# Layer 3's attention: a head's scores on 64 rows in one pass, heads two at a time, operands stacked through device memory, four attentions issued as one stream

## The chip, the core and the metric

The kernel runs on one core of one Trainium2 chip. The metric is the device time of one launch in microseconds. A core has a matrix engine (TensorE, PE in the profile; its weight loads are PEld), a vector engine (VectorE, DVE), a scalar engine (ScalarE, ACT), GpSimd (POOL), and a queue that issues transfers (SyncE, SP). Each engine works through its own instructions in order; semaphores tie them together. On-chip memory is SBUF, the matrix engine writes to PSUM, and device memory is HBM.

## The reference

Four layers in a row are added to a tensor `x` of 2 x 128 x 64 x 64 in float32; each takes the group-normalised tensor. Layers 0 to 2 (an attention with a channel attention, a convolution mix, a quaternion Fourier layer) are the same before and after. Layer 3 is a plain self-attention over the 4096 positions, with 8 heads of 16 channels, for each of the two batch entries:

```python
    xf = x.reshape(B, C, S)                      # 2, 128, 4096
    q, k, v = proj(wq, bq), proj(wk, bk), proj(wv, bv)   # each B, 8, 16, S
    a = jnp.einsum('bhcq,bhck->bhqk', q, k) / jnp.sqrt(jnp.float32(C))
    a = jax.nn.softmax(a, axis=-1)
    o = jnp.einsum('bhqk,bhck->bhcq', a, v)
    return o.reshape(B, C, h, w)                 # added to x
```

## The kernel before, in words

**The work of layer 3.** It is cut into four attentions: batch entry `b` (0, 1) times a set `t` (0, 1) of four heads, `j` = 0 to 3. In each, the queries are cut into 8 blocks `qb` of 512 columns (`CH`, `NCH`) and the keys into 32 tiles `kt` of 128 (`NQT`). One step is one (`qb`, `kt`): there are 256 steps in an attention and 1024 in the layer. A step is

- `scores` (L2102): for every head a 128 x 512 block of scores into PSUM, keys on the partitions. Two PSUM tiles `ps_s` hold it, heads 0 and 1 in the first, heads 2 and 3 in the second. There are three such tiles in the pool (`f3_sp`, `bufs=3`), so a step's pair shares a buffer with its neighbours;
- two exponentials on ScalarE (L2112), 128 x 1024 each, from `ps_s` to `weights` in SBUF;
- `multiply` (L2121): for every head `weights` times the 32 columns of `vt` (16 channels of values and 16 of ones, whose sums are the softmax's denominators), four heads beside each other in 32-column strips of the array, summed over `kt` in one PSUM tile `ps_acc`. It runs two steps behind `scores`.

At the last `kt` of a block `done` (L2141 to L2154) transposes, divides, adds the residual and writes out.

**How a score is split.** Scores are computed in the fast float32 form of TensorE (`F32R`, "fp32r" in the profile) from rounded parts, so that nothing is lost. A head has 32 rows: 16 channels twice. In `k` the upper copy holds the rounded key and the lower one its remainder (`hi`, `sign`, `upper`); in `q[0]` both copies hold the rounded query, in `q[1]` its remainder. Head `j` sits on rows 32j to 32j+31, so four heads work side by side in the array, and a step takes two passes: all four heads with `q[0]`, then all four with `q[1]`, added up in PSUM.

**Around it.** `folded` folds the normalisation of batch entry `b` into the weights (its statistics by `_group_stats_pow`). `queries_and_keys` makes `q` and `k` by pieces of 512 columns: a matmul (L2030), then seven VectorE operations; for the first two pieces of all, three of them are on ScalarE. `values` (L2056, L2063) makes `vt` in 8 pieces, each 4 matmuls and one VectorE addition. `bound` takes the largest query and key for a flag, checked at the end of the kernel.

**What sets the order.** Inside layer 3 `_in_order` keeps PE, DVE, ACT and POOL in the order of the program text; the SP queue is ordered by the framework's scheduler. The first attention starts when two pieces of queries, keys and values are there; the other pieces follow inside its first block, one at every second `kt` (`early`). Each attention carries the preparation of the next one beside it (`beside`): one piece at `kt` = 4, 12 and 20 of a block, 16 pieces with a matmul each or four, and some more without. An attention ends with `for x in waiting: multiply(*x)`, then the next one begins.

Of the kernel before, what the change touches and what calls it, by code (L numbers as in the profile page):

```python
# [1288 lines left out]
F32R = mybir.dt.float32r  # L1289
ENGINES = (  # L1290
# [672 lines left out]
def _layer3(ctx, tc, X, l3, cst, out, worst, here):  # L1963
# [10 lines left out]
    def acc():  # L1974
        return accp.tile([128, CH], F32, tag="acc", name="ps_acc")
# [11 lines left out]
    def folded(b, got):  # L1987

        x = X[:, b, :]
        if b:  # L1990
            mean, rstd = _group_stats_pow(nc, two, acc, x, cst, mhalf)
        else:
            mean, rstd = here[:, 0:1], here[:, 1:2]
        yield
# [24 lines left out]
    def queries_and_keys(b, t, f, q, k, idle):  # L2019

        wqk, _, bqk, _ = f
        bq, bk, bk2 = (bqk[:, n, t : t + 1] for n in range(3))
        for c in range(NCH):
            cols = slice(c * CH, (c + 1) * CH)
            ps = acc()
            nc.tensor.matmul(ps, wqk[:, t, :], X[:, b, cols], start=True, stop=True)  # L2030

            qq = two.tile([128, CH], F32, tag="qq", name="qq", bufs=1)
            nc.vector.stream_shuffle(qq, ps, OF_Q)  # L2033
            kk = two.tile([128, CH], F32, tag="kk", name="kk", bufs=1)
            nc.vector.stream_shuffle(kk, ps, OF_K)  # L2035
            hi = two.tile([128, CH], F32R, tag="hi", name="hi", bufs=1)
            if c < idle:
                nc.scalar.activation(hi, kk, AF.Identity, bias=bk)
                nc.scalar.activation(kk, kk, AF.Identity, bias=bk2, scale=upper)  # L2039
                nc.scalar.activation(q[0][:, cols], qq, AF.Identity, bias=bq)  # L2040
            else:
                nc.vector.tensor_scalar_add(hi, kk, bk)
                nc.vector.tensor_scalar(kk, kk, bk, upper, ALU.add, ALU.mult)
                nc.vector.tensor_scalar_add(q[0][:, cols], qq, bq)
            nc.vector.scalar_tensor_tensor(k[:, cols], hi, sign, kk, ALU.mult, ALU.add)
            nc.vector.scalar_tensor_tensor(
                q[1][:, cols], qq, bq, q[0][:, cols], ALU.add, ALU.subtract
            )
            yield
# [20 lines left out]
    def bound(b, t, q, k):  # L2070


        top = two.tile([128, 2, 2], F32, tag="top", name="top")
        for n, x in enumerate((q[0], k)):
            for i in range(2):
                nc.vector.tensor_reduce(
                    top[:, n, i : i + 1],
                    x[:, i * S // 2 : (i + 1) * S // 2],
                    AX.X,
                    ALU.max,  # L2080
                    apply_absolute_value=True,
                )
                yield
        m = two.tile([128, 2], F32, tag="m", name="m")
        nc.vector.tensor_reduce(m, top, AX.X, ALU.max)
        mm = two.tile([128, 1], F32, tag="mm", name="mm")
        nc.vector.scalar_tensor_tensor(mm, m[:, 0:1], lower, m[:, 1:2], ALU.mult, ALU.mult)
        ps = acc()
        nc.tensor.matmul(ps[:, 0:1], head_sum, mm, start=True, stop=True)  # L2089
        n = 1 + 2 * b + t  # L2090
        nc.vector.tensor_scalar_mul(worst[:, n : n + 1], ps[:, 0:1], 1.02)
        yield

    def attend(b, t, q, k, vt, early):
        ac = [None]

        def scores(qb, kt):
            ps = [spp.tile([128, 2, CH], F32, tag="sp", name="ps_s") for _ in range(2)]
            for n in range(2):
                for j in range(4):  # L2100
                    rows = slice(32 * j, 32 * j + 32)
                    nc.tensor.matmul(  # L2102
                        ps[j // 2][:, j % 2, :],
                        k[rows, kt * 128 : (kt + 1) * 128],
                        q[n][rows, qb * CH : (qb + 1) * CH],
                        start=(n == 0),
                        stop=(n == 1),
                    )
            w = []
            for p in range(2):  # L2110
                w.append(pp.tile([128, 2, CH], F32, tag="weights", name="weights"))
                nc.scalar.activation(w[p], ps[p], AF.Exp)  # L2112
            return w

        def multiply(qb, kt, w):
            if kt == 0:
                ac[0] = acc()
            for j in range(4):

                i = j % 2  # L2120
                nc.tensor.matmul(  # L2121
                    ac[0][32 * j : 32 * j + 32, :],
                    vt[:, kt, j // 2, i : i + 2, :].rearrange("p a d -> p (a d)"),
                    w[j // 2][:, i, :],
                    start=(kt == 0),
                    stop=(kt == NQT - 1),
                )
            if kt == NQT - 1:
                done(qb, ac[0])

        def done(qb, ps):
            cols = slice(qb * CH, (qb + 1) * CH)

            places = [
                (slice(32 * j + 16 * (j % 2), 32 * j + 16 * (j % 2) + 16),
                 slice(64 * t + 16 * j, 64 * t + 16 * j + 16))
                for j in range(4)
            ]
            xs = residual[qb % 2]
            for to, rows in places:  # L2140
                nc.sync.dma_start(xs[to, :], X[rows, b, cols])  # L2141
            z = two.tile([128, CH // 32, 32], F32, tag="z", name="z", bufs=1)
            flat = z.rearrange("p n i -> p (n i)")
            nc.vector.transpose(flat, ps)  # L2144
            r = two.tile([128, CH // 32], F32, tag="r", name="r")
            for j in range(4):
                rows = slice(32 * j, 32 * j + 32)
                nc.vector.reciprocal(r[rows, :], z[rows, :, 16 * (1 - j % 2)])  # L2148
            nc.vector.tensor_mul(z, z, r.unsqueeze(2).to_broadcast([128, CH // 32, 32]))
            u = two.tile([128, CH], F32, tag="u", name="u", bufs=1)  # L2150
            nc.vector.transpose(u, flat)
            nc.vector.tensor_add(u, u, xs)
            for at, rows in places:
                nc.sync.dma_start(out[b, rows, cols], u[at, :])  # L2154

        waiting = []
        for qb in range(NCH):
            for kt in range(NQT):
                if kt % 2 == 0:
                    over = next(early, early) is early  # L2160
                waiting.append((qb, kt, scores(qb, kt)))
                if len(waiting) > 2:
                    multiply(*waiting.pop(0))
                yield kt if over else None
        for x in waiting:
            multiply(*x)
# [10 lines left out]
    def work():  # L2177

        for b in range(B):
            f = []  # L2180
            yield from folded(b, f)
            for t in range(2):
                first = b == 0 and t == 0
                q = [two.tile([128, S], F32R, tag=f"q{n}", name=f"q{n}") for n in range(2)]
                k = two.tile([128, S], F32R, tag="k", name="k")
                vt = two.tile([128, NQT, 2, 3, 16], F32, tag="vt", name="vt")
                early = values(b, t, f, vt)
                keys = queries_and_keys(b, t, f, q, k, 2 * first)
                if first:

                    for _ in range(2):
                        next(keys)
                        next(early)
                        yield
                    early = in_turn(keys, early)
                else:
                    for _ in early:
                        yield
                    yield from keys
                yield b, t, (q, k, vt, early)  # L2200
                yield from bound(b, t, q, k)

    def up_to_next(side):
        for x in side:
            if x:
                found.append(x)
                return
            yield

    side = work()  # L2210
    found = []
    for _ in up_to_next(side):
        pass
    while found:
        b, t, got = found.pop()
        beside = up_to_next(side)
        for kt in attend(b, t, *got):

            if kt in (4, 12, 20):
                next(beside, None)  # L2220
        for _ in beside:
            pass


def _input(nc, X, a, b):
    for i in range(4):
# [127 lines left out]
```

## Time and profile before

| what | value |
|---|---|
| median of 3 runs | 4194.57 us (4191.61 to 4198.47) |
| the profiled execution's own time | 4192.35 us |
| its span | 4190.2 us |
| layer 3 in it: first exponential to the end of the last | 2233.1 to 4178.0 us |
| exponentials of layer 3 | 2048, busy 1884.9 us, idle before them 61.0 us |
| PE busy over the span | 96% |
| ACT busy over the span | 80% |

How to read the profile: the busy time of an engine is the union of its instructions' times, so that 2048 exponentials of 1101 ns each, which overlap a little, are busy for 1884.9 us. A matmul's end is modelled, and matmuls overlap, so that a busy PE says nothing of how much of it is needed; what it waits for is read from its weight loads (PEld). "idle before" with an arrow is the time for which the engine stood still before such instructions, and what came last to release it. In the timeline "x8" means eight instructions of a kind in a row, and a time in brackets is the idle time before the first of them.

### The profile page before, as it was taken

Reading aid. Unit: us, or ns where it says so; the run is one execution under the profiler, and the core shown is the slowest. Engines: PE = TensorE matmul, PEld = TensorE weight load, DVE = VectorE, ACT = ScalarE, POOL = GpSimd, SP = SyncE. Lnnn points to the kernel's source line nnn. Section 1 sums busy time; section 2 is a strip of 40 time slices with the busy share of each in tenths; the row PEclk is TensorE's granted clock in tenths of the full one; section 3 lists DMA queues with packets and bytes.
Section 4 is the critical chain, followed back from the end, with each engine's and each line's share of the span. In section 5 each row is a group of like instructions: output and inputs, shape, how many; then the busy total and the mean of one; then the engine's idle time right before and its main releaser. Section 6 shows DMA issues by size and latency. Waiting matters only on the chain. (4 is left out here: it accounts for less than half of the span.)

```text
span 4190.2 us, 90476 instructions
## 1 busy us (share of the span) xinstructions
PE 4027.6 (96%) x39886; PEld 1505.7 (36%) x39886; DVE 2088.3 (50%) x2454; ACT 3333.8 (80%) x4035; POOL 71.7 (2%) x145
## 2 busy tenths in 40 slices
PE   7999999989999998997999999999999999999998
PEld 4522222354222224445664333333333333333333
DVE  4689999767899998895754102221022102210000
ACT  4478888735888883326646999999999999999998
POOL 1001000000000001000000000000000000000000
PEclk9999999999999999998989999999999999999999
DMA  1199970000000000004640000000000000000000
GB/s 49 26 185 181 179 98 1 2 2 2 1 2 2 2 2 12 1 15 190 271 195 4 6 6 6 4 6 6 4 6 6 6 4 6 6 4 6 6 6 5
DMA packets 158855, 159.39 MB, mean 38 GB/s; under 512 B 24809, under 2 KB 148713, under 8 KB 154354
## 3 DMA queue, kind: packets, MB, share of 16 engines
q1 hardware_dynamic: 158450, 153.50, 15.7%
q8 instruction: 314, 5.14, 0.5%
q14 instruction: 91, 0.75, 0.1%
HBM read 145.09 MB, written 73.40 MB: 52 GB/s over the span
## 5 line engine op out<-in xcount | busy, mean ns | idle before, releaser
L2112 ACT ACTIVATE weights<-ps_s 128x1024 f32<-128x1024 f32 x2048 | 1884.9, 1101 | 61.0 <-PE ps_s L2102 60.6
L1352 ACT ACTIVATE weights<-ps_s 128x1024 f32<-128x1024 f32 x1024 | 993.1, 1023 | 167.9 <-PE ps_s L1343 149.7
L2121 PE MATMUL ps_acc<-weights,vt 128*32 128x512 f32 x8192 | 1093.2, 606 | 0.0
L2102 PE MATMUL ps_s<-q,k 32*128 32x512 f32 x8192 | 924.1, 444 | 5.4 <-ACT weights L2112 5.4
L1800 DVE TENSOR_TENSOR sums<-sums,weights 128x2048 f32<-128x2048 f32 x384 | 880.0, 2292 | 42.6 <-ACT weights L1352 6.4
L2102 PEld LDWEIGHTS ps_s<-q,k 32*128 32x128 f32 x8192 | 471.2, 182 | 839.7 <-ACT weights L2112 773.1
L1343 PE MATMUL ps_s<-q,k 32*64 32x512 f32 x8192 | 629.9, 613 | 4.6 <-ACT weights L1352 2.4
L1760 PE MATMUL ps_acc<-weights,vt 128*32 128x512 f32 x4096 | 550.0, 605 | 7.2 <-ACT used L1790 3.7
L2144 DVE STREAM_TRANSPOSE z<-ps_acc 128x512 f32<-128x512 f32 x32 | 22.9, 717 | 1064.6 <-PE ps_acc L2121 1064.6
L1343 PEld LDWEIGHTS ps_s<-q,k 32*64 32x64 f32 x8192 | 161.5, 129 | 433.9 <-PE ps_s L1343 337.9
L2121 PEld LDWEIGHTS ps_acc<-weights,vt 128*32 128x32 f32 x8192 | 162.9, 108 | 378.6 <-issue 375.4
L1760 PEld LDWEIGHTS ps_acc<-weights,vt 128*32 128x32 f32 x4096 | 81.2, 108 | 426.7 <-issue 403.2
L662 DVE SCALAR_TENSOR_TENSOR X<-g,w,X 128x2048 f32<-128x2048 f32 x84 | 197.4, 2351 | 2.6
L1800 DVE TENSOR_TENSOR sums<-weights 128x2048 f32<-128x2048 f32 x64 | 146.6, 2291 | 63.0 <-ACT weights L1352 62.6
L1548 PE MATMUL ps_sp<-pad,diag 32*32 32x512 f32 x4608 | 158.9, 597 | 2.3 <-ACT q L1568 1.3
L1008 PE MATMUL ps_z<-w_ri,e 128*32 128x128 f32 x2048 | 137.5, 409 | 14.5 <-DVE e L950 12.3
L2063 DVE TENSOR_TENSOR vt<-ps_acc,bv 128x384 f32<-128x384 f32 x32 | 17.8, 557 | 264.7 <-PE ps_acc L2056 264.7
L2033 DVE LOAD_MASK_SELECT qq<-ps_acc x32 | 0.4, 14 | 239.0 <-PE ps_acc L2030 239.0
L1548 PEld LDWEIGHTS ps_sp<-pad,diag 32*32 32x32 f32 x4608 | 95.5, 103 | 53.6 <-issue 15.6
L950 DVE TENSOR_SCALAR e<-ps_pe 32x136 f32<-32x136 f32 (+1 forms) x352 | 104.4, 297 | 4.9
L948 ACT ACTIVATE e<-ps_pe 32x136 f32<-32x136 f32 (+1 forms) x352 | 99.3, 282 | 4.1
L710 PE MATMUL ps_bank<-t,t 128*128 128x512 f32 x224 | 101.3, 610 | 0.0
(288 smaller groups left out, 2488.6 us busy)
## 6 DMA issues: line engine op xcount, KB each, us to landing
w_ri<-w_r SPq DMA_DIRECT2D x16, 2112.0 KB, 8.1
w_ri<-w_i SPq DMA_DIRECT2D x16, 2112.0 KB, 13.4
w_r<-in_L_conv_kr_w SPq DMA_DIRECT2D x15, 528.0 KB, 13.1
w_r<-in_L_conv_kr_x SPq DMA_DIRECT2D x15, 528.0 KB, 12.9
w_r<-in_L_conv_kr_y SPq DMA_DIRECT2D x15, 528.0 KB, 12.9
w_r<-in_L_conv_kr_z SPq DMA_DIRECT2D x15, 528.0 KB, 12.9
w_i<-in_L_conv_ki_w SPq DMA_DIRECT2D x15, 528.0 KB, 13.3
w_i<-in_L_conv_ki_x SPq DMA_DIRECT2D x15, 528.0 KB, 12.7
```

Of the source, the lines that this page charges most:

```text
L662: nc.vector.scalar_tensor_tensor(xi, g[:, i : i + H // 2, j : j + W], w8[:, s : s + 1], xi, ALU.mult, ALU.add)
L710: nc.tensor.matmul(ps.rearrange("p (h w) -> p h w", w=W), t9[:, k, :], t2[:, c * ROWS + k : (c + 1) * ROWS + k, 2 : W + 2], start=(k == 0) ...
L950: nc.vector.tensor_scalar_mul(out, got[of, :, s], sign)
L1008: nc.tensor.matmul(out.rearrange("p (n f o) -> p n f o", n=2, f=2), e[:, s, 2 * j : 2 * j + 2, :].rearrange("p f x -> p (f x)"), w.rearran ...
L1343: nc.tensor.matmul(ps[j // 2][to, j % 2, :], k[rows, kt * 128 + 64 * half : kt * 128 + 64 * half + 64], q[rows, qb * CH : (qb + 1) * CH], ...
L1352: nc.scalar.activation(w[:, 2 * p : 2 * p + 2, :], ps[p], AF.Exp)
L1548: nc.tensor.matmul(ps[r // 2][to, r % 2, :].rearrange("p (h w) -> p h w", w=W), diag[rows, grp, t, :], pad[rows, y0 : y0 + ROWS, t % 3 : t ...
L1760: nc.tensor.matmul(ac[n][rows, :], lhs(rows), w[:, j, :], start=first, stop=last)
L1800: nc.vector.tensor_add(parts[0].rearrange("p j c -> p (j c)"), t.rearrange("p j c -> p (j c)"), w.rearrange("p j c -> p (j c)"),)
L2102: nc.tensor.matmul(ps[j // 2][:, j % 2, :], k[rows, kt * 128 : (kt + 1) * 128], q[n][rows, qb * CH : (qb + 1) * CH], start=(n == 0), stop= ...
L2112: nc.scalar.activation(w[p], ps[p], AF.Exp)
L2121: nc.tensor.matmul(ac[0][32 * j : 32 * j + 32, :], vt[:, kt, j // 2, i : i + 2, :].rearrange("p a d -> p (a d)"), w[j // 2][:, i, :], star ...
```

## The change

The parts, with the names of the diff:

1. `scores`: a head's 64 rows (16 channels, times two parts of the query, times two parts of the key) are multiplied in one pass. Rows 0 to 63 and 64 to 127 take a head each, so two heads work at a time: heads 0 and 1, then heads 2 and 3. A step has 4 score matmuls of 64 rows instead of 8 of 32 rows, and 4 weight loads of 64 x 128 instead of 8 of 32 x 128. Every matmul starts and stops its own sum.
2. `queries_and_keys` writes each piece's three 128 x 512 tiles (`q[0]`, `q[1]`, `k`) to device memory (3 transfers of 256 KB), and `stacked` reads them back so that the rows of `q[0]` and `q[1]` alternate and those of `k` stand twice: 8 transfers of 64 rows x 512 (128 KB each). Queries and keys are held as 8 + 8 single tiles of 128 x 2 x 512 instead of two sets of three 128 x 4096 tiles; the next attention's tiles take the places of those which the present one has finished with (`laid`).
3. The maximum for `bound` is taken piece by piece inside `queries_and_keys` (2 reductions of 512 columns for each piece) instead of 4 reductions of 2048 afterwards.
4. The four attentions run as one stream: `waiting` goes on across them, so that the last multiplies of one come after the first scores of the next. Preparation is laid at `kt` = 3, 6, ..., 30 of a block (`SIDE`), taking `others` (bound, fold, values, statistics) and `keys` in turn. A piece of queries and keys is four such turns, of which only the first has a matmul. `keys` of the next attention begin in its second block. The statistics of the second batch entry come by `_stats_steps`.
5. An exponential on VectorE (`exponentials`) is written, but `BY_VECTOR` is empty, so it is not used, and `ORDER` is the plain order.

```diff
-    def queries_and_keys(b, t, f, q, k, idle):
...
-                nc.vector.tensor_scalar_add(q[0][:, cols], qq, bq)
-            nc.vector.scalar_tensor_tensor(k[:, cols], hi, sign, kk, ALU.mult, ALU.add)
-            nc.vector.scalar_tensor_tensor(
-                q[1][:, cols], qq, bq, q[0][:, cols], ALU.add, ALU.subtract
+    def queries_and_keys(g, c, idle):
...
+        nc.vector.stream_shuffle(kk, ps, OF_K)
+        yield
+        k = two.tile([128, CH], F32R, tag="ks", name="ks", bufs=1)
+        q = [two.tile([128, CH], F32R, tag=f"qs{n}", name=f"qs{n}", bufs=1) for n in range(2)]
...
+        yield
+        nc.vector.scalar_tensor_tensor(k, k, sign, kk, ALU.mult, ALU.add)
+        nc.vector.scalar_tensor_tensor(q[1], qq, bq, q[0], ALU.add, ALU.subtract)
+        for n, x in enumerate((q[0], q[1], k)):
+            to = dram.tile([128, CH], F32, name=f"stack{2 * b + t}_{c}_{n}")
+            nc.sync.dma_start(to, x.bitcast(F32))
+            g.kept[c, n] = to
+        yield
+        for n, x in enumerate((q[0], k)):
+            nc.vector.tensor_reduce(
+                top[:, n, c : c + 1], x, AX.X, ALU.max, apply_absolute_value=True
             )
-            yield
+        yield
+
+    def stacked(g, c, name, parts):
+
+        to = one.tile([128, 2, CH], F32R, tag=f"{name}{c}", name=f"{name}{c}")
+        for n, part in enumerate(parts):
+            for p in range(2):
+                nc.sync.dma_start(
+                    to[n::2, p, :].bitcast(F32), g.kept[c, part][64 * p : 64 * p + 64, :]
+                )
+        getattr(g, name)[c] = to
...
-            for n in range(2):
-                for j in range(4):
-                    rows = slice(32 * j, 32 * j + 32)
-                    nc.tensor.matmul(
-                        ps[j // 2][:, j % 2, :],
-                        k[rows, kt * 128 : (kt + 1) * 128],
-                        q[n][rows, qb * CH : (qb + 1) * CH],
-                        start=(n == 0),
-                        stop=(n == 1),
-                    )
...
+    def scores(g, qb, kt):
+        ps = [spp.tile([128, 2, CH], F32, tag="sp", name="ps_s") for _ in range(2)]
+        keys = slice(kt % 4 * 128, kt % 4 * 128 + 128)
+        for j in range(4):
+            rows = slice(64 * (j % 2), 64 * (j % 2) + 64)
+            nc.tensor.matmul(
+                ps[j // 2][:, j % 2, :],
+                g.k[kt // 4][rows, j // 2, keys],
+                g.q[qb][rows, j // 2, :],
+                start=True,
+                stop=True,
+            )
...
-        for kt in attend(b, t, *got):
-
-            if kt in (4, 12, 20):
-                next(beside, None)
-        for _ in beside:
...
+    def attended(g, early, others, following):
+
+        after, over, keys = None, False, iter(())
+
+        def laid(qb, kt):
+
+            for name, parts, free in (("q", (0, 1), qb), ("k", (2, 2), kt // 4 if qb == NCH - 1 else 0)):
+                c = len(getattr(after, name))
+                if c < free and (c, 2) in after.kept:
+                    stacked(after, c, name, parts)
+
+        for n in range(NCH * NQT):
+            qb, kt = divmod(n, NQT)
+            if kt % 2 == 0:
+                over = next(early, early) is early
+            next(chain[0], None)
+            scores(g, qb, kt)
+            waiting.append((g, qb, kt))
+            if len(waiting) > LAG:
+                multiply(*waiting.pop(0))
+            if after:
+                laid(qb, kt)
+            if not over or kt not in SIDE:
+                continue
+            if SIDE.index(kt) % 2 == 0:
+                next(others, None)
+                continue
+            if after is None and following and qb:
+                for _ in others:
+                    pass
+                after, others = following()
+                keys = chained(*after.keys)
+            next(keys, None)
...
+    def first_laid(keys, g):
+
+        for c in range(NCH):
+            yield from keys[c]
+            stacked(g, c, "q", (0, 1))
+            stacked(g, c, "k", (2, 2))
+
+    f = []
+    run(folded(0, here, f))
+    g = Group(0, 0, f, 2)
+    keys = in_pieces(first_laid(g.keys, g), 4)
+    for c in range(2):
+        next(keys)
+        next(g.values)
+    early = in_turn(keys, g.values)
```

## The prediction

> **What bounds the kernel now.** I read the groups of instructions first, then busy time by attention, then the timeline in a quiet stretch and around a piece of preparation, and last the start of layer 3. The change touches only layer 3, so nothing before 2220 us should move.
>
> ```profile
> L2112 ACT ACTIVATE weights<-ps_s 128x1024 f32<-128x1024 f32 x2048 | 1884.9, 1101 | 61.0 <-PE ps_s L2102 60.6
> L2121 PE MATMUL ps_acc<-weights,vt 128*32 128x512 f32 x8192 | 1093.2, 606 | 0.0
> L2102 PE MATMUL ps_s<-q,k 32*128 32x512 f32 x8192 | 924.1, 444 | 5.4 <-ACT weights L2112 5.4
> ```
>
> ScalarE is the bound: 2048 exponentials, idle for 61.0 us, all but 0.4 of it waiting for scores. PE looks busier (1093.2 + 924.1), but these are overlapping, modelled times. The windows, ACT's exponentials alone, one row for each attention (columns: stretch, length, busy and count, granted clock, DMA share, GB/s):
>
> ```profile
> 2233.00:2733.00 500.00, 475.75 (x516) 1.00 0.02 5
> 2733.00:3222.00 489.00, 471.04 (x513) 1.00 0.02 6
> 3222.00:3710.00 488.00, 471.32 (x513) 1.00 0.02 6
> 3710.00:4178.00 468.00, 466.78 (x509) 1.00 0.02 6
> ```
>
> Idle: 24, 18, 17 and 1 us. The last attention, which prepares no successor, loses nothing; the others lose it to preparation, and the first also to its own start.
>
> ```profile
> 3899.08 5.71 ACT L2112 ACTIVATE weights<-ps_s 128x1024 f32<-128x1024 f32 x6
> ...
> 3900.08 0.47 PEld L2102 LDWEIGHTS ps_s<-q,k 32*128 32x128 f32 x8 [0.84 <-ACT weights L2112]
> ...
> 3900.92 0.16 PEld L2121 LDWEIGHTS ps_acc<-weights,vt 128*32 128x32 f32 x8 [0.37 <-issue]
> ...
> 3901.92 0.47 PEld L2102 LDWEIGHTS ps_s<-q,k 32*128 32x128 f32 x8 [0.84 <-ACT weights L2112]
> ```
>
> Quiet: a step takes 1.833 us (two exponentials at a pitch of 0.917). Scores start at 3900.08, and the exponential that needs them at 3899.08 + 2 x 0.917 = 3900.91, 0.83 later. So PE has no lead. Now a stretch with one piece:
>
> ```profile
> 2239.53 1.13 PE L2030 MATMUL ps_acc<-X,wqk 128*128 128x512 f32 x2
> 2240.59 0.30 PEld L2102 LDWEIGHTS ps_s<-q,k 32*128 32x128 f32 x8 [0.76 <-ACT weights L2112]
> 2241.26 0.16 PEld L2121 LDWEIGHTS ps_acc<-weights,vt 128*32 128x32 f32 x8 [0.37 <-issue]
> 2241.42 3.77 ACT L2112 ACTIVATE weights<-ps_s 128x1024 f32<-128x1024 f32 x4 [0.85 <-PE ps_s L2102]
> 2242.25 0.54 PEld L2102 LDWEIGHTS ps_s<-q,k 32*128 32x128 f32 x8 [0.84 <-issue]
> ...
> 2729.53 7.44 ACT L2112 ACTIVATE weights<-ps_s 128x1024 f32<-128x1024 f32 x8 [1.87 <-PE ps_s L2102]
> ```
>
> A piece occupies PE for 1.06 us (2239.53 to 2240.59). Unhindered scores take 0.67 (to 2241.26), the multiply 0.99 (to 2242.25): PE needs 1.66 of 1.83, 0.17 to spare. The exponential came 0.85 late. The last row is the seam between two attentions.
>
> The loss to be won: from 2233.13 to 4177.96 are 1944.8 us, less 1024 x 1.833 = 1877: 68 us. Pieces: 3 x 16 at 0.97 = 47 (0.85 idle, and some 0.1 because exponentials no longer overlap). The first block: 12 pieces, one at every second step, about 13. The seams, 3 x 2.3: 7. Sum 67.
>
> **The change, part by part.**
>
> *Scores.* PE time: before, two passes of four heads, 0.67, so 0.335 for one. After, two passes of two heads with 512 columns each. No row shows a matmul on 64 rows. Nearest is the 32-row pass, 0.335; the low end is 0.30, for fewer loads; the high end, if two heads don't overlap, is four times 0.335 = 1.34 a step. I take 0.67: the time is in the columns. [...] all eight loads, the second pass's on the same rows, were over in 0.30, while matmuls of 0.44 mean ran. [...]
>
> *What is gained is the lead.* Before, both PSUM tiles were complete only after the second pass, 0.83 after the start, and both had to be free for the first pass to finish. After, heads 0 and 1 finish in the first pass: their exponential can start at 0.83 - 0.335 = 0.50; I take 0.59, since a first pass also waits for its weights. The second tile need only be free when the second pass starts. Let e be the start of an exponential: its tile is free at e + 1.17 (1.12 for the late exponentials and a semaphore), the second pass starts at e + 1.28, PE is through at e + 1.615, the multiply at e + 2.605, and the next pair's first exponential could start at e + 3.195. ScalarE reaches it at e + 4 x 0.917 = e + 3.667. Lead: 0.47, before 0.
>
> So a piece of 1.06 costs ScalarE 0.59 instead of 0.97. The lead comes back at 0.17 a step, so in three steps: the smallest distance in `SIDE`. 48 x 0.59 = 28. In the first block pieces come every second step and 0.34 is rebuilt: 12 x 0.72 = 9. Together 37.
>
> *One stream.* At a seam the next scores precede the last multiplies: 7 becomes 0. Bound, fold and statistics have matmuls of 0.3 to 0.4 a turn and fit the lead.
>
> Exponentials win 68 - 37 = 31 us.
>
> *Stacks, at the start.* This is what the change adds to the path.
>
> ```profile
> 2221.70 4.97 SPq L2141 DMA_DIRECT2D residual<-X  x8
> ...
> 2231.87 1.57 PE L2102 MATMUL ps_s<-q,k 32*128 32x512 f32 x10
> ...
> 2233.13 7.44 ACT L2112 ACTIVATE weights<-ps_s 128x1024 f32<-128x1024 f32 x8 [1.11 <-PE ps_s L2102]
> ```
>
> The transfers nearest in size (KB each, median us from issue to landing):
>
> ```profile
> out<-u SPq DMA_DIRECT2D x128, 32.0 KB, 1.7
> ...
> w_k<-in_L_conv_wk SPq DMA_DIRECT2D x1, 128.0 KB, 2.1
> ```
>
> SP takes 0.62 to issue one (4.97 / 8), [...] I take 0.5. The first piece's `q[1]` is ready at 2228.1 (L2046 at 2227.32, 0.74 long). A 256 KB store: above the 2.1 of 128 KB, say 2.4; the last, issued by 2228.9, has landed at 2231.3. Eight loads from 2229.7 on, one every 0.5: issued by 2233.7, landed 2.1 later at 2235.8. Scores start 3.9 later than 2231.87, the first exponential some 3 later, since it needs one pass only. The next piece's `ks`, `qs` wait for stores to have left: 1 more. Cost 4. PE does a piece (1.06) meanwhile, inside this wait: back 1. Net 3; ends 2 and 20.
>
> The upper end is the loop in the first block: every four steps a piece goes through SP, 3 stores, landing, 8 loads. At 0.5 and 2.4 about 8 us, against 4 x 1.66 + 2 x 1.06 = 8.8 for PE: hidden. At 0.62 and 4.7 (the 512 KB input's landing) it is 11.5: 2.7 late, six times, 16.
>
> *Costed at nothing.* Later stacks: SP has a block of 58.7 us for about 11 transfers more, and tiles are asked for at least 20 us ahead of use; 56 MB over 1900 us is 30 GB/s, where earlier stages of this kernel moved 190 to 270. SP is in order, so `out` and `residual` stand behind stores that wait for VectorE and loads that wait for PE to leave a tile; the residual is asked for a block ahead and `u` is needed a block later. Were that cover gone, `done` would hold VectorE, with it `ps_acc`, and then a piece on PE. Reductions by pieces: 16 of about 0.6 instead of 4 of 2.28 an attention, on a VectorE busy 84 of 489 us. The tail after the last exponential is the same.
>
> Sum: 31 - 3 = 28. The profiled execution took 4192.35 (span 4190.2 and 2.2 around it), so 4164.4; it lies 2.2 below the median of the runs shown. I say 4165.
>
> **Rivals.**
>
> *No lead (0.12).* The first exponential still starts only at 0.83, because the passes finish together or the semaphore comes late. Then seams are won (7) and part of the second tile's wait; pieces cost about 0.8: 48 x 0.8 + 12 = 50, 68 - 50 - 3 = 15: 4179. For it: 491 ns long first-pass matmuls. Against: half of a step's scores are then really done.
>
> *The loop of stacks binds the first block (0.12).* 16 to 25 of the 31 go: 4180 to 4190. For it: 0.62 an issue, one queue. Against: transfers of 128 KB took 2.1.
>
> *Two heads don't run side by side (0.07): slower.* Then a step's scores take more than 0.84, PE needs more than 1.833, and ScalarE waits in every step; all is lost from about 0.86 on. [...] One after the other, 1.34: +500. For it: no 64-row matmul is in the trace. Against: column strips (L2121) and 32-row strips both overlap here.
>
> *The forecast (0.69)*: 4165, own range 4155 to 4176.
>
> **How the numbers follow.** Faster by over 0.2% (8.4 us, about what a measurement of this kernel can tell from no change): forecast, no lead, and half of the loop: 0.69 + 0.12 + 0.05 = 0.86. Same: the other half of the loop, 0.06. Slower: 0.07, and 0.01 for a worse loop: 0.08. The range reaches from 4151 (passes of 0.28) to 4186, and leaves out the slower cases and the end of the loop.
>
> **What would show it.** Right: exponential idle falls from 61 to about 35; seam waits of 1.87 gone; waits of a piece about 0.5 instead of 0.85; L2102's successor has 4096 matmuls; first exponential near 2236; scores to multiply 0.67 when unhindered. Wrong: scores waiting for a `q` or `k` landing inside a block, idle in every step, or VectorE holding a piece's `ps_acc`.

## The result, and the profile after

The changed kernel took 4159.34 us (median of 4 runs, 4158.50 to 4159.76) against 4195.78 us before: ratio 0.9914, 95% interval 0.9897 to 0.9931. Measured again later beside the kernel before, it took 4165.25 us (5 runs, 4159.20 to 4166.09) against 4190.39: ratio 0.9936, interval 0.9922 to 0.9950. Why the medians of one kernel lie several us apart is told with the experiments; by the profiles of layer 3 the change itself is worth 26 to 29 us. The profiled execution took 4159.76 us, its span 4157.9.

The groups of the changed kernel (exponentials, scores, and the weight loads of the scores):

```profile
L2181 ACT ACTIVATE weights<-ps_s 128x1024 f32<-128x1024 f32 x2048 | 1884.2, 1354 | 33.6 <-PE ps_s L2167 33.6
L2167 PE MATMUL ps_s<-q,k 64*128 64x512 f32 x4096 | 896.8, 490 | 2.5 <-DMA k<-stack 2.5
L2167 PEld LDWEIGHTS ps_s<-q,k 64*128 64x128 f32 x4096 | 372.2, 183 | 1015.5 <-ACT weights L2181 1007.5
```

Idle before exponentials fell from 61.0 to 33.6 us. Half as many score matmuls keep PE busy for nearly the same time (896.8 for 924.1). A sign to learn: an exponential's record is now 1354 ns long in the mean instead of 1101, at the same pitch. No exponential got slower: 2048 records of 1354 ns come to 2773 us, but they cover 1884.2 us, so most open before the one ahead has closed. Read so, a record can open only when its scores are there, and the longest record makes the lead visible. The mean doesn't: behind a piece the records grow from 1.02 us by some 13 ns each and reach 1.58 us only 43 exponentials later, yet a piece three steps behind another (2316.90 after 2310.87) costs 0.54 us, hardly more than the 0.50 of one that stands alone, so PE has its lead back long before. Minimum, median and maximum of a record's ns were 1018, 1117 and 1130 before; after:

```profile
L2181 ACT ACTIVATE weights<-ps_s x2048: 1014/1392/1588, 2230.7 to 4143.1; 128x1024 f32<-128x1024 f32 x187
```

The windows, exponentials alone, by attention:

```profile
2230.00:2718.00 488.00, 472.35 (x513) 0.99 0.19 59
2718.00:3197.00 479.00, 471.44 (x514) 1.00 0.12 36
3197.00:3675.00 478.00, 471.15 (x513) 1.00 0.12 36
3675.00:4145.00 470.00, 469.22 (x512) 1.00 0.03 7
```

Idle is 16, 8, 7 and 1 us where it was 24, 18, 17 and 1. Now a quiet step and a piece in the timeline:

```profile
2453.96 0.19 PEld L2167 LDWEIGHTS ps_s<-q,k 64*128 64x128 f32 x2 [0.84 <-ACT weights L2181]
...
2454.36 0.19 PEld L2167 LDWEIGHTS ps_s<-q,k 64*128 64x128 f32 x2 [0.22 <-ACT weights L2181]
2454.80 0.16 PEld L2190 LDWEIGHTS ps_acc<-weights,vt 128*32 128x32 f32 x8 [0.24 <-issue]
...
2455.79 1.13 PE L2048 MATMUL ps_acc<-X,wqk 128*128 128x512 f32 x2
2456.85 0.30 PEld L2167 LDWEIGHTS ps_s<-q,k 64*128 64x128 f32 x4 [0.76 <-ACT weights L2181]
...
2457.45 1.94 ACT L2181 ACTIVATE weights<-ps_s 128x1024 f32<-128x1024 f32 x2 [0.39 <-PE ps_s L2167]
2457.51 0.16 PEld L2190 LDWEIGHTS ps_acc<-weights,vt 128*32 128x32 f32 x8 [0.37 <-issue]
```

In the quiet step the loads come two and two: the second pair of heads waits until ScalarE has freed its tile (2454.36), while the first pair is on its way; before, all eight loads stood in one row. After the piece (2455.79 to 2456.85, 1.06 us as before) the four loads come together, and scores take 2456.85 to 2457.51 = 0.66. The exponential waits 0.39 us where it waited 0.85.

From here on the loss of a kernel is worked out from the records: end of the last exponential, less end of the first, less 2047 times the quiet pitch of 0.9166. It counts lost pitch, not idle time, so it does not depend on overlaps. Before: 67.5 us. After: 36.7 us. A piece beyond the first block costs 0.96 before and 0.49 to 0.55 after.

The start of layer 3 (SP, PE and ACT):

```profile
2223.34 2.46 SPq L2084 DMA_DIRECT2D q<-stack  x4
...
2225.84 2.51 SPq L2084 DMA_DIRECT2D k<-stack  x4
...
2229.86 2.70 PE L2167 MATMUL ps_s<-q,k 64*128 64x512 f32 x8 [2.54 <-DMA k<-stack]
...
2230.69 3.77 ACT L2181 ACTIVATE weights<-ps_s 128x1024 f32<-128x1024 f32 x4 [3.71 <-PE ps_s L2167]
```

Eight loads took 0.62 us each to issue, and one landed 2.5 to 2.6 us after its issue in the median; PE waited for the last, and began with a granted clock of 0.58 on average over the next 12 us.

### The profile page after: what moved, and what is told of

It is laid out like the page before. It is cut to its first block, busy times and chain, and to the rows that moved or that the text cites. A ratio compares the mean times of both kernels' runs of the same rounds, so it can differ in the third digit from the quotient of the medians.

```text
span 4157.9 us, 82928 instructions
## 1 busy us (share of the span) xinstructions
PE 3993.2 (96%) x35790; PEld 1401.6 (34%) x35790; DVE 2088.9 (50%) x2502; ACT 3332.1 (80%) x4035; POOL 71.6 (2%) x145
## 5 line engine op out<-in xcount | busy, mean ns | idle before, releaser
L2181 ACT ACTIVATE weights<-ps_s 128x1024 f32<-128x1024 f32 x2048 | 1884.2, 1354 | 33.6 <-PE ps_s L2167 33.6
L2167 PE MATMUL ps_s<-q,k 64*128 64x512 f32 x4096 | 896.8, 490 | 2.5 <-DMA k<-stack 2.5
L2167 PEld LDWEIGHTS ps_s<-q,k 64*128 64x128 f32 x4096 | 372.2, 183 | 1015.5 <-ACT weights L2181 1007.5
## 6 DMA issues: line engine op xcount, KB each, us to landing
w_ri<-w_i SPq DMA_DIRECT2D x16, 2112.0 KB, 13.3
```

Of the source, the lines that this page charges most:

```text
L2167: nc.tensor.matmul(ps[j // 2][:, j % 2, :], g.k[kt // 4][rows, j // 2, keys], g.q[qb][rows, j // 2, :], start=True, stop=True,)
L2181: nc.scalar.activation(w[0], ps[p], AF.Exp)
```

## The experiments

Each is an edit of the changed kernel. The numbers of the profiles, in one table; "start" is where layer 3's first instruction on GpSimd begins (`head_sum`), "to first" is from there to the first exponential, "loss" as worked out above.

| kernel | start, us | to first, us | loss, us | median, us |
|---|---|---|---|---|
| before | 2220.2 | 13.0 | 67.5 | 4195.78 |
| before, again | 2213.7 | 13.3 | 68.1 | 4187.56 (one run) |
| after | 2213.3 | 17.4 | 36.7 | 4159.34 |
| after, again | 2216.6 | 16.3 | 36.3 | 4165.25 |
| old scores | 2210.1 | 14.9 | 63.4 | 4188.48 |
| pairs late | 2220.0 | 17.2 | 48.7 | 4177.31 |
| pairs cut | 2217.7 | 16.4 | 36.7 | 4160.56 |
| half pieces | 2213.2 | 16.2 | 19.6 | 4143.26 |
| half pieces, again | 2219.1 | 16.2 | 19.4 | 4141.44 |
| seams | 2213.5 | 17.0 | 41.2 | 4169.01 |
| direct | 2222.1 | 14.0 | 36.3 | 4158.58 |
| half and direct | 2212.2 | 13.5 | 22.3 | 4141.04 |

The medians were taken in several rounds, on different chips (the later ones on chips 14, 7 and 8), and the kernel before, measured in each, had 4194.73, 4194.78 and 4190.39; the ratios below are each to the kernel before of the same round.

**Old scores: one part undone.** Theory: the gain is the lead. Rivals: it is the stream and the place of the pieces, or the smaller number of score instructions.

```diff
-        for j in range(4):
-            rows = slice(64 * (j % 2), 64 * (j % 2) + 64)
+        for n in range(2):
+            for j in range(4):
+                rows = slice(32 * j, 32 * j + 32)
...
-                g.k[kt // 4][rows, j // 2, keys],
-                g.q[qb][rows, j // 2, :],
-                start=True,
-                stop=True,
+                    g.k[kt // 4][rows, 0, keys],
+                    g.q[qb][rows, n, :],
+                    start=(n == 0),
+                    stop=(n == 1),
```

> The changed kernel with the scores put back: eight matmuls of 32 rows in two passes of four heads (the stored pieces are read back as they are, 3 loads of 256 KB a piece instead of 8 of 128 KB); stream, order and tiles are those of the change. Theory (the gain is the lead of PE over ScalarE that the new scores give): the lead is gone, a piece costs ScalarE 0.96 us again instead of 0.50, and in the second and third block pieces lie closer than before; idle of the exponentials from 37 to 63 us, some 2 us back at the start for fewer loads; 4185 us. Rival 1 (the gain is the stream and the place of the pieces): about 4160 to 4165. Rival 2 (the gain is that PE has fewer score instructions to work through): 4180 or more too; the pair of the next two kernels tells it from the theory.

Measured 4188.48 us (12 runs; 4185 was expected), ratio to the kernel before 0.9989, interval 0.9981 to 0.9998. The loss is 63.4 us. The page's row and two rows of a quiet step in its timeline:

```profile
L2179 ACT ACTIVATE weights<-ps_s 128x1024 f32<-128x1024 f32 x2048 | 1884.4, 1103 | 58.4 <-PE ps_s L2165 58.0
```

```profile
2701.50 0.47 PEld L2165 LDWEIGHTS ps_s<-q,k 32*128 32x128 f32 x8 [0.84 <-ACT weights L2179]
...
2702.34 0.16 PEld L2188 LDWEIGHTS ps_acc<-weights,vt 128*32 128x32 f32 x8 [0.37 <-issue]
```

The records are short again (1103), the idle time is back, and the step is that of the kernel before. Stream and place alone give 4 of the 31 us of loss (7 at the seams and in the small turns of bound, fold and statistics, less 3 that the first block loses more); the rival of placement falls. The other rival doesn't yet, since this kernel also has eight score matmuls a step.

**Pairs late, pairs cut: the same eight matmuls in two orders.** The edit of pairs late; pairs cut has the loop over `p` outside the one over `h`.

```diff
-        for j in range(4):
...
+        for h in range(2):
+            for p in range(2):
+                cut = slice(h * CH // 2, (h + 1) * CH // 2)
+                for i in range(2):
+                    rows = slice(64 * i, 64 * i + 64)
+                    nc.tensor.matmul(ps[p][:, i, cut], g.k[kt // 4][rows, p, keys],
+                                     g.q[qb][rows, p, cut], start=True, stop=True)
```

> The changed kernel with every score matmul cut in two of 256 columns, laid so that both pairs of heads end late: first half of pair 0, first half of pair 1, second half of pair 0, second half of pair 1. Eight matmuls a step as before the change, the same columns. Theory of the lead: the first pair ends after three quarters instead of one half, and its last quarter must wait until the second tile is free, so the lead is all but gone: the exponentials wait some 18 us longer, 4177 us. Rival 2 (number of instructions): the same time as the other order of the same eight matmuls.

> The same eight matmuls of 256 columns, laid pair by pair: both halves of pair 0, then both halves of pair 1. Theory of the lead: as the changed kernel, 4159 to 4162 us, since pair 0 is done at the same point. Rival 2 (number of instructions): clearly above 4165 us, most of the way to the kernel before.

Late: 4177.31 us (5 runs), loss 48.7. The time is the one expected, but in part by luck: the loss rose by 12 us, not by 18, since a piece costs 0.74 here and some lead is left. Cut: 4160.56 us (4 runs), loss 36.7, the changed kernel's own. The exponentials' line of each, late first (minimum, median and maximum of a record's ns):

```profile
L2184 ACT ACTIVATE weights<-ps_s x2048: 1017/1170/1179, 2237.2 to 4162.1; 128x1024 f32<-128x1024 f32 x187
```

```profile
L2184 ACT ACTIVATE weights<-ps_s x2048: 1015/1370/1587, 2234.0 to 4146.4; 128x1024 f32<-128x1024 f32 x187
```

Same instructions, same bytes, only the order differs: the longest record is 1179 ns where the first pair ends late, and 1587 where it ends at half time (the medians mix in the growth behind each piece). The number of instructions is no cause; the point at which the first tile is complete, and the second is needed, is.

**Half pieces: what a lead can hide.**

```diff
-        for kt in range(0, NQT, 4):
+        m = 4 if b == 0 and t == 0 else 2
+        for kt in range(0, NQT, m):
...
-        nc.tensor.matmul(ps, wqk[:, t, :], X[:, b, cols], start=True, stop=True)
+        n = CH if b == 0 and t == 0 else CH // 2
+        for at in range(0, CH, n):
+            ps = acc()
+            cols = slice(c * CH + at, c * CH + at + n)
+            nc.tensor.matmul(ps[:, :n], wqk[:, t, :], X[:, b, cols], start=True, stop=True)
...
+            yield
```

> The changed kernel with the pieces of preparation of the second to fourth attention cut in halves: values by 2 key tiles instead of 4, the matmul of queries and keys by 256 columns in two turns (so a piece is still four turns: stores and maximum share one). The work is the same but for one more vector operation for each half. Theory of the lead: half a piece takes PE 0.53 to 0.6 us, about the lead of 0.56, and three steps rebuild it, so it costs ScalarE almost nothing; of the 24 us that 48 pieces cost, some 20 come back: 4138 us. Rival (a piece costs ScalarE its PE time less a fixed share, however it is cut): no change, 4159; rival (each interruption has a price of its own): slower, up to 4175.

4143.26 us (4 runs, 4141.14 to 4148.69), ratio to the kernel before 0.9885, interval 0.9868 to 0.9901. Loss 19.6 us; outside the first block of all some 10. Its page's row, and two half pieces in its timeline with the scores that follow each:

```profile
L2184 ACT ACTIVATE weights<-ps_s 128x1024 f32<-128x1024 f32 x2048 | 1886.4, 1271 | 13.9 <-PE ps_s L2170 13.8
```

```profile
2314.83 0.69 PE L2097 MATMUL ps_acc<-wv,X 128*128 128x96 f32 x4
2315.44 0.30 PEld L2170 LDWEIGHTS ps_s<-q,k 64*128 64x128 f32 x4
...
2320.42 0.70 PE L2052 MATMUL ps_acc<-X,wqk 128*128 128x256 f32 x2
2321.05 0.30 PEld L2170 LDWEIGHTS ps_s<-q,k 64*128 64x128 f32 x4 [0.33 <-ACT weights L2184]
```

A half takes PE 0.61 to 0.63 us (2314.83 to 2315.44, 2320.42 to 2321.05), so two halves take 1.24 instead of 1.06, and still 17 of the 24 us that pieces cost are gone: each half nearly fits the lead. A piece has no price of its own; what it has beyond the lead is what ScalarE pays. The time expected was 4138 and 4143 was measured; the loss fell by 17 and not by 20 because a half is longer than half a piece: it exceeds the lead of 0.56 by some 0.06, and each of the 96 halves costs 0.07 in the median.

**Seams: the stream cut at the ends of the attentions.**

```diff
+        while waiting:
+            multiply(*waiting.pop(0))
         if after:
             run(keys)
```

> The changed kernel with the stream cut at the ends of the attentions: the last multiplies of one come before the first scores of the next, as before the change; all else as changed. By the prediction's sum a seam costs 1.5 to 2.3 us even with the lead used up, three of them 5 to 6: exponentials lose 42 instead of 37 us, and nothing else moves; the time is 4164 to 4165 us, hardly to be told from 4159 in the times, but the profile shows three waits of 1.5 us or more at the seams. Rival (the seams' tail is hidden by the lead now): 37 us as in the changed kernel.

4169.01 us (6 runs, 4160.46 to 4175.33); loss 41.2 us. The first seam among its exponentials:

```profile
2718.27 5.60 ACT L2181 ACTIVATE weights<-ps_s 128x1024 f32<-128x1024 f32 x6 [1.64 <-PE ps_s L2167]
```

Three seams of 1.75 us of lost pitch each, as expected, and about 1 us more after the first two and none after the third; in the changed kernel 0.6 us are lost there after each. By the losses the seams are worth 4.5 us with the new scores, or 5.6 without the first block of all, which happened to lose 1.1 less here; they were put at 7 with the old ones. In the times this can't be told: the medians, 4169 and 4159 or 4165, scatter by more.

**Direct: the first attention stacked from SBUF to SBUF.** The unstacked pieces have two buffers, and `g.kept` holds them instead of a tensor in device memory. The loads also stand one turn earlier in the program, before the maxima; these two parts of the edit are left out below.

```diff
+            if b == 0 and t == 0:
+                g.kept[c, n] = x.bitcast(F32)
+                continue
             to = dram.tile([128, CH], F32, name=f"stack{2 * b + t}_{c}_{n}")
             nc.sync.dma_start(to, x.bitcast(F32))
```

> The changed kernel, but the first attention's pieces are stacked from SBUF to SBUF, without device memory (8 transfers a piece instead of 3 + 8; two buffers for the unstacked pieces). By the timeline of the changed kernel the loads of the first piece began at 2223.3, 2.3 us after its first store was issued; without the round trip the first exponential comes some 2.4 us sooner after the start of layer 3 (15.0 instead of 17.4 us), and PE stands idle for shorter at the start, so that the three slow steps there shrink from 3.5 to below 3 us of loss; together 2.5 to 3.5 us, below what the times can tell. Rival (the issue of eight loads on one queue is the start's price, not the round trip): no change in the first exponential's place.

4158.58 us, as the changed kernel within what the times can tell. In the profile the first exponential comes 14.0 us after the start, 3.4 earlier than in the changed kernel's first profile and 2.3 earlier than in its second; the loss is 36.3. Of the 3 to 4.5 us by which the first exponential came later than before, some 2.5 went with the round trip through device memory. That the second buffers and the earlier place of the loads have no part in it was not tested; but the changed kernel's first store was issued at 2221.01 and its first load at 2223.34, 2.3 us later. The first three losses of the block are 2.4 us in sum for the 3.5 of the changed kernel's first profile; the seams kernel, with an unchanged start, had 2.4 too, so this is within what runs differ by.

**Half and direct**, with the loads of the first two heads issued first:

> Both together: pieces cut in halves for the second to fourth attention, and the first attention stacked from SBUF to SBUF with the loads of the first pair of heads issued first. Exponentials lose 18 to 19.5 us as with halves alone, and the first one comes 3 to 5 us sooner: some 4 us below the kernel with halves, 4139 us, about 55 below the kernel before.

4141.04 us (4 runs, 4140.47 to 4147.95), ratio to the kernel before 0.9878, interval 0.9864 to 0.9893. The first exponential came at 13.5, 2.7 us sooner, but the loss is 22.3, not below 19.5. So what was gained at the start was given back: 1.5 us inside the first block (11.0 lost where half pieces alone lost 9.5), where PE waited 2.0 us for a stacked query, the rest in small losses of the later blocks. So this is no better than half pieces alone, and both beat the changed kernel.

**Before again, after again, half pieces again.** The median gain of the first measurement, 36 us, is more than layer 3 shows.

> The kernel before, once more, for its profile. In the two profiles layer 3 began at 2220.2 us before and at 2213.3 us after, though nothing ahead of it was changed. If that is a matter of the run, this profile puts it somewhere between 2210 and 2221 again, and layer 3 itself takes the same 1957 us from its start to the last exponential's start within 1 us; if the change had moved it, it is 2220 again.

> The changed kernel once more. Two profiles of the kernel before had layer 3 begin at 2220.2 and 2213.7 us, the one of the changed kernel at 2213.3; from there to the last exponential the two kernels differ by 27 us. If the start of layer 3 is a matter of the run for both kernels alike, more runs of the changed kernel spread over 4157 to 4168 and their median comes to some 4160 to 4166, 28 to 34 below the kernel before. If the change moved the earlier layers too, all of them stay at 4158 to 4160 and the profile again has layer 3 begin at 2213.

> The kernel with halved pieces once more, beside the changed kernel on the same chip: 17 us less loss of the exponentials in the profiles and 1 us less at the start, so 16 to 19 us below the changed kernel, 4141 to 4148 us.

The first of these rows is the kernel before in its first profile, the second the same kernel again; in the changed kernel the row begins at 2213.26:

```profile
2220.15 0.20 POOL L1365 MEMSET head_sum<- 128x128 f32 x1 [4.93 <-PE ps_po L1147]
```

```profile
2213.66 0.20 POOL L1365 MEMSET head_sum<- 128x128 f32 x1 [3.99 <-PE ps_po L1147]
```

Layer 3 began at 2210 to 2222 us in twelve profiles, and one and the same kernel began it at 2213.7 and at 2220.2: what the layers ahead of it take is a matter of the run. Where before and after began layer 3 at the same point (2213.7 and 2213.3), their spans were 4185.4 and 4157.9: 27.5 us apart. Where they didn't, 32.3. After again: 4165.25 us, in the spread that was expected if the start is a matter of the run; it lies 25 below the kernel before beside it, where 28 to 34 were expected. From the start of layer 3 to the last exponential ("to first" and "loss" together) each of the two profiles before exceeds each of the two after by 26.4 to 28.8 us. Half pieces again: 4141.44 us, ratio to the kernel before 0.9882, interval 0.9867 to 0.9897; 24 below the changed kernel in the medians, where 16 to 19 were expected and the two profiles' losses differ by 17.

## Why the prediction was right

The mechanism was right: the new scores give PE a lead, and the lead hides part of every piece. The total was also right because errors in its parts cancelled.

*Scores.* Taken as 0.67 for two passes of two heads; measured 0.66: a pass of 64 rows by 512 columns takes 0.33, where one of 32 rows took 0.335. In the row at 2456.85 all four loads, the second pair's on the rows of the first, are over in 0.30, while matmuls of 0.50 run, as all eight were in the row at 2240.59 of the kernel before.

*Lead.* Taken as 0.47; the records of 1.58 us in quiet stretches against 1.02 for an exponential that finds nothing ahead of it give 0.56, and so does a piece's 1.06 on PE less the 0.50 that it costs. A piece was put at 0.59. Old scores take the lead away and pairs late shorten it; the first brings 27 of the 31 us of loss back, the second 12. That is shown.

*Loss by parts,* from the records, us:

| part | before, put at | before | after, put at | after | old scores | pairs late | half pieces |
|---|---|---|---|---|---|---|---|
| first block of all | 13 | 9.6 | 9 | 9.8 | 12.5 | 9.6 | 9.5 |
| the other 48 pieces | 47 | 46.0 | 28 | 24.3 | 46.1 | 35.6 | 7.6 |
| seams and small turns | 7 | 11.9 | 0 | 2.5 | 4.8 | 3.5 | 2.5 |
| sum | 67 | 67.5 | 37 | 36.7 | 63.4 | 48.7 | 19.6 |

*The first block* was to win 4 us and won nothing. Before, two of its twelve pieces cost nothing and ten cost 0.96. After, nine losses of 0.71 to 0.72 came as forecast, but the first three were 0.93, 1.19 and 1.35.

*The pieces* won 22 us instead of 19, since the lead is longer than forecast.

*Seams and small turns* won 9 us instead of 7. The seams themselves came to nothing, as forecast. But that bound, fold and statistics "fit the lead" was wrong by 2.5 us: `bound` cost 0.57 to 0.58 in the second to fourth attention, and a fold 0.82. The fold holds PE for 1.38 us (two groups of matmuls with VectorE between them, 2735.67 to 2737.05). `bound` has 0.38 us of matmul, but near the start of an attention VectorE is still at `done` of the one before, and PE, in order, waits for it with all scores behind:

```profile
2724.92 0.30 PEld L2115 LDWEIGHTS ps_acc<-mm,head_sum 128*128 128x128 f32 x2 [1.66 <-DVE mm L2113]
```

The exponential behind it waited 0.47 us. In the first attention the same turn found its operand ready and cost nothing. The 7 us of the seams count the waits of the kernel before; with the new scores and the seams kept, 41.2 - 36.7 = 4.5 would be lost.

*Start.* A net cost of 3 was predicted. The first exponential comes 4.4 us later after the start of layer 3 in one pair of profiles and 3.0 in the other. The first three losses of the block add 1.3 us to this in the first profile and 1.0 in the second (the table counts them in the first block); with them the start cost 4 to 6 us. The issue of a load was taken as 0.5 us and took 0.62; a 256 KB store was taken as 2.4 and landed in 2.1 to 2.3.

*Sum.* 31 - 3 = 28 predicted; 27.5 in the pair of profiles that began layer 3 at the same point, 26.4 to 28.8 by layer 3 alone in all four pairs. The medians are 4159.34 and 4165.25, the forecast was 4165. What the first measurement has beyond the sum is not in layer 3, as far as the profiles show. The prediction took the 2.2 us between the profiled execution and the median as all that runs differ by: the start of layer 3 alone moves by 12 us. That the runs without a profile differ for the same reason was not shown, since only the profiled ones tell where layer 3 begins. So how close the medians lie to the forecast is in part luck.

*Rivals.* "No lead" expected 4179; nearest to its case are pairs late, 4177, where a piece costs 0.74 and some lead is left, and old scores, 4188, where it costs 0.96. The loop of stacks did not bind the first block: from its fourth loss on each piece costs 0.71 to 0.72. Two heads do run side by side: a step's four score matmuls, each 0.39 to 0.50 us long in the row at 2456.85, took 0.66 together.

## What to carry to other kernels

When one engine feeds another through few buffers, ask not only how long a step of the feeder takes but when its first buffer is complete and when its last one must be free; work that finishes one buffer after the other gave a lead of 0.56 us at no cost here, work that fills all buffers together gave next to none (0.10, a piece's 1.06 less the 0.96 that it cost). Side work on the feeder costs what exceeds the lead, so cut it to the size of the lead, space it so that the lead can grow back, and lay it where its operands are ready: a wait for another engine counts as side work too. When single runs of long unchanged stages differ by as much as the effect, compare the stage itself in the profiles, not the totals.

## What the runs showed of the hardware that was not expected

PE starts the changed kernel's scores (2229.86) with a granted clock of one half. The clock fell before the wait for the stacks, not in it. The first row below is PE's pause ahead of that wait, the others are windows (columns: stretch, length, busy time of PE, PEld, DVE, ACT and POOL with counts, granted clock, DMA share, GB/s):

```profile
2223.54 2.02 PE L2094 MATMUL ps_acc<-wv,X 128*128 128x96 f32 x8 [3.58 <-DVE vt L2101]
```

```profile
2219.00:2222.00 3.00, 0.96 (x2) 0.13 (x2) 1.59 (x3) 1.96 (x3) 0.00 (x0) 1.00 0.15 40
2222.10:2229.80 7.70, 3.78 (x10) 2.21 (x10) 6.07 (x14) 2.15 (x3) 0.00 (x0) 0.50 0.74 232
2229.90:2239.00 9.10, 9.09 (x36) 4.21 (x40) 5.26 (x11) 6.41 (x7) 0.00 (x0) 0.50 0.66 216
```

PE stood still from 2219.96 to 2223.54, waiting for VectorE, and the clock, 1.00 up to 2222.0, was at half from 2222.1 on, some 2 us into this pause. It stayed there through the wait for the stacks and for 9 us of work after it; from 2239.2 on it was 1.00. In the kernel before, the scores started at 2231.87; the clock was 0.50 until 2233.2 and 1.00 from 2233.3 on.

What the low clock costs is not shown. It fits that the first eight score matmuls took 2.70 us and the first three losses were large. But in half pieces, whose first attention is laid in the same way, the clock was 1.00 from 2233.2 on, 4.4 us after its first scores, and its first three losses still came to 3.1 us, for 3.5 in the changed kernel. There PE waited 1.65 us for VectorE, which had waited for a store of `ks`, held in a single buffer:

```profile
2233.67 0.49 DVE L2063 TENSOR_SCALAR ks<-kk,bqk 128x512 fp32r<-128x512 f32 x1 [3.91 <-DMA stack<-ks]
```

VectorE waits for that store in the changed kernel too, for 3.5 us. How the three losses divide between store and clock stays open.
